# A graph layer on one core: index preparation and rows of h moved into the first pass, and nine passes of other sizes in place of seven

## The chip, the core and the metric

The kernel runs on one core of one Trainium2 chip. The metric is the device time of one execution in microseconds. PE is the matrix engine, DVE the vector engine, ACT the scalar engine, POOL the GpSimd engine; SP only issues DMAs here. PE, DVE, ACT and SP each run a list in the order in which it was written; a DMA that an engine issues stands in that list too.

## What is computed

```python
def _L0_gnn_ref(x, f_ij, rcut_ij, idx_i, idx_j, W_in2f, W_f1, b_f1, W_f2, b_f2, W_o1, b_o1, W_o2, b_o2):
    def smu(x, alpha=0.01, mu=2.5):
        return ((1 + alpha) * x + (1 - alpha) * x * erf(mu * (1 - alpha) * x)) / 2
    h = x @ W_in2f.T
    Wij = smu(f_ij @ W_f1.T + b_f1) @ W_f2.T + b_f2
    Wij = Wij * rcut_ij[:, None]
    x_ij = h[idx_j] * Wij
    agg = jax.ops.segment_sum(x_ij, idx_i, num_segments=h.shape[0])
    out = smu(agg @ W_o1.T + b_o1) @ W_o2.T + b_o2
    return out
h = jnp.maximum(_layernorm(x, axis=-1), 0.0)
x = x + _L0_gnn_ref(h, edge_attr_20, edge_weight, src, dst, ...)
```

There are 12,500 nodes with 128 features, 400,000 edges with 20 features each, and everything is float32. dst (idx_j, the node whose row of h is read) comes sorted; src (idx_i, the node that the message is added to) is random.

## The kernel before

The nodes lie in 98 bins of 128 (NB). The edges lie in 3125 tiles of 128 (NT), four of which are a group (GRP, 782 groups), eight a supertile (SUP, 391 of them). The supertiles are divided into passes by PARTS (line 32), six of 59 and one of 37; the code calls a pass an epoch. Every pass has a buffer of its own in DRAM with CAP slots for each bin: the mean number of edges that fall into a bin plus 5.8 standard deviations, rounded up to 128. Q is CAP / 128: 6 for a pass of 59, 4 for one of 37. Slots from ZMIN on may stay unused, and are filled with zeros beforehand (clear, line 152).

For a group of four tiles the loop does this. load (line 367) fetches for each supertile the edge features, the row of relative dst indices (rel_dram, which the kernel wrote itself) and 128 rows of h from h_dram. h is kept as three bfloat16 parts. bins, count, read and number find for each edge the slot in the bin of its src. hide, bend, smooth and weigh are the filter network. pick, gather and take read the rows of h through a one-hot matrix, mix multiplies the two, turn transposes, and send scales by the edge weight and scatters the messages: one indirect DMA on POOL for each tile (line 562), 3125 in all, each of 128 rows of 129 floats.

While pass k scatters, pass k-1 is summed. begin and fetch (lines 624 and 576) read the buffer back in chunks of up to 12 times 128 slots on SP's queue, choose (line 587) makes a one-hot matrix for a chunk on DVE, and add (line 598) does one 128 x 128 x 128 matrix product for each bin and each of its Q parts and adds four bins at once into agg. Here such a product is called a sum; it stands as two matrix instructions in the profile. begin comes with the second group of a pass, the first choose with its third, the first sums with its fifth (WAIT, line 634), and the sums of a pass are spread evenly over its other groups. DVE, PE and ACT wait in order, so what stands behind a choose waits with it. Meanwhile the buffer of the next pass is cleared from SP's queue, in about 50 DMAs.

After the last group the last pass has nothing to run beside: its 98 bins are summed, and for each unit of four bins the output network runs (half and rest, lines 318 to 341), with x read again and the result written from ACT's queue. rest of a unit comes in the middle of the next four bins, half at their end.

Ahead of the loop stands the preparation (lines 216 to 313): all of dst, src and the weights come in whole, on ACT's queue; the rest of x comes on POOL's. rel is made for all tiles, transposed on PE and written to rel_dram; hi_b and lo_b (bin and place in the bin of each src) are made for all edges; and the first eight bins (HEAD, line 168) get layer norm, ReLU and the product with W_in, so that their rows of h stand in h_dram. The dst of the first pass lie in these bins. The rows of the other 90 bins are made inside the first pass: others (line 661) yields steps, and step takes one at three places of every group (two statistics and two empty steps in turn, then the deviations, then six steps for every four bins).

A message tile ms has six buffers, so ACT and DVE may run up to six groups ahead of POOL.

Of the kernel before, what the change touches and what calls it, by code (L numbers as in the profile page):

```python
# [11 lines left out]
I32 = mybir.dt.int32  # L12
# [19 lines left out]
PARTS = (59, 59, 59, 59, 59, 59, 37)  # L32
# [7 lines left out]
def gnn_kernel(  # L40
# [85 lines left out]
    nc.vector.memset(onesb, 1.0)  # L126
    bad = const.tile([P, 4 + 2 * EPOCHS], F32, name="bad")
    nc.vector.memset(bad, 0.0)
# [39 lines left out]
    HEAD = 8  # L168
# [47 lines left out]
    with tc.tile_pool(name="prep", bufs=1) as prep, \  # L216
            tc.tile_pool(name="node", bufs=3) as node, \
            tc.tile_pool(name="nps", bufs=2, space=PSUM) as nps:
        dst_i = prep.tile([P, NT], I32, name="dst_i")
        src_i = prep.tile([P, NT], I32, name="src_i")  # L220
        nc.scalar.dma_start(dst_i, dst_col)
        nc.vector.memset(x_sb[:, NB - 1, :], 0.0)
        nc.sync.dma_start(x_sb[:, 0:HEAD, :], bin_rows(x, 0, HEAD))
        nc.sync.dma_start(w_in, w_in_t)
        for a, n in chunks(NB - 1 - HEAD, 30):
            nc.gpsimd.dma_start(x_sb[:, HEAD + a:HEAD + a + n, :], bin_rows(x, HEAD + a, n))
        nc.gpsimd.dma_start(x_sb[:LASTB, NB - 1, :], x[(NB - 1) * P:N, :])
        nc.scalar.dma_start(src_i, src_col)
        nc.scalar.dma_start(w_sb, w_col)
        nc.vector.memset(w_f1, 0.0)  # L230
        nc.scalar.dma_start(w_f1[0:R, :], w_f1_t)
        nc.scalar.dma_start(w_f1[R:R + 1, :], b_f1)
        nc.scalar.dma_start(w_f2, w_f2_t)
        nc.scalar.dma_start(w_o1, w_o1_t)
        nc.scalar.dma_start(w_o2, w_o2_t)
        nc.scalar.dma_start(b1, b_o1.rearrange("o p -> p o"))
        nc.scalar.dma_start(b2row, b_f2)
        nc.scalar.dma_start(b2, b_f2.rearrange("o p -> p o"))
        nc.scalar.dma_start(bo2, b_o2.to_broadcast([P, P]))

        nc.vector.memset(zero, 0.0)
        clear(0, len(cleans) - 1, nc.sync)
        zero_b = prep.tile([P, 3 * D], BF, name="zero_b")
        nc.vector.memset(zero_b, 0.0)
        nc.scalar.dma_start(h_dram[NB * P:N + WIN, :], zero_b[:N + WIN - NB * P, :])


        nc.vector.tensor_copy(base_i[:, :], dst_i[0:1, 0:NT:SUP])
        base_f = prep.tile([1, NS], F32, name="base_f")
        nc.vector.tensor_copy(base_f, base_i)  # L250
        rel = prep.tile([P, NT], F32, name="rel")
        nc.vector.tensor_copy(rel, dst_i)
        S = GRP * P // SUP
        for a, n in chunks(NS, S):
            pb = nps.tile([P, S, SUP], F32, name="pb")
            nc.tensor.matmul(pb[:, :n], ones1, base_f[:, a:a + n].unsqueeze(2).to_broadcast([1, n, SUP]),
                             start=True, stop=True)
            w = min(NT - a * SUP, n * SUP)
            nc.vector.tensor_sub(rel[:, a * SUP:a * SUP + w], rel[:, a * SUP:a * SUP + w],
                                 pb.rearrange("p s t -> p (s t)")[:, :w])  # L260
        for a, m in chunks(NT // P, GRP) + [(NT // P, 0)]:
            pd = nps.tile([P, GRP, P], F32, name="pd")
            rb = node.tile([P, GRP, P], BF, name="rb")
            if m:
                for j in range(m):
                    nc.tensor.transpose(pd[:, j, :], rel[:, (a + j) * P:(a + j + 1) * P], ident)
                nc.scalar.activation(rb[:, :m], pd[:, :m], AF.Copy)
                nc.sync.dma_start(rel_dram[0, a * P * P:(a + m) * P * P].rearrange("(c t e) -> t c e", t=P, e=P),
                                  rb[:, :m])
            elif NT % P:  # L270
                m = NT % P
                nc.tensor.transpose(pd[:m, 0, :], rel[:, a * P:NT], ident)
                nc.scalar.activation(rb[:m, 0], pd[:m, 0], AF.Copy)
                nc.sync.dma_start(rel_dram[0, a * P * P:].rearrange("(t e) -> t e", e=P), rb[:m, 0])
        lh = prep.tile([P, 2], F32, name="lh")
        nc.vector.tensor_reduce(lh[:, 0:1], rel, op=ALU.min, axis=AX.X)
        nc.vector.tensor_reduce(lh[:, 1:2], rel, op=ALU.max, axis=AX.X)
        nc.vector.tensor_scalar(bad[:, 0:1], lh[:, 0:1], 0.0, None, op0=ALU.is_lt)
        nc.vector.tensor_scalar(bad[:, 1:2], lh[:, 1:2], float(WIN - 1), None, op0=ALU.is_gt)
        most = prep.tile([1, 1], F32, name="most")  # L280
        early = eps_of[0][1] + 3
        nc.vector.tensor_reduce(most, base_f[:, :early], op=ALU.max, axis=AX.X)
# [13 lines left out]
        for b in range(HEAD):  # L296
            stats(node, b)
# [45 lines left out]
    with tc.tile_pool(name="ld", bufs=4) as ld, \  # L343
# [291 lines left out]
        for s in range(3):  # L635
            load(s)
        for s in range(2):
            pick(s)
# [266 lines left out]
```

## Time and profile before

| | us |
|---|---|
| three runs: median (lowest, highest) | 4286.98 (4285.12, 4287.03) |
| the profiled execution, its own time | 4295.33 |
| its span, first to last instruction | 4293.6 |
| first scatter starts | 93.53 |
| last scatter starts | 4094.83 |

| engine | busy us | share of the span |
|---|---|---|
| PE | 3745.7 | 87% |
| DVE | 3177.7 | 74% |
| POOL | 3029.8 | 71% |
| ACT | 2825.2 | 66% |

A row of groups reads: line, engine, operation, what is written from what, times how often, then busy time, mean duration in ns, and the idle time before it with its main cause. A row in order of time reads: start, duration, engine, line, operation, and in brackets how long the engine had been idle and what ended that. A row of stretches reads: from:to, length, then busy time and number of instructions for PE, PE's weight loads, DVE, ACT and POOL, the clock granted to PE, the busy share of the DMA engines and GB/s. POOL's time does not count what lies between two of its DMA instructions. DMA issues are printed with a q behind the engine's name.

### The profile page before, as it was taken

The page shows a single profiled execution, that of the slowest core. Times are in us where ns is not written, and L with a number is a line of the kernel's source. Part 1 is how long each engine was busy: PE and PEld are TensorE (multiplying, and loading weights), DVE is VectorE, ACT ScalarE, POOL GpSimd, SP SyncE. Part 2 cuts the span into 40 slices and gives each one's busy share as a digit, 9 for nine tenths or more (in the row PEclk, how much of TensorE's full clock was granted, in tenths as well). Part 3 has the DMA queues.
Part 4 walks back from the last instruction along what each step waited for, and adds up shares of the span by engine and source line. Part 5 has one row for each costly group of instructions (what it writes and reads, how often), then busy time and mean ns, then how long its engine had stood idle before and what let it go on. Part 6 is the DMA issues. An engine that isn't in the chain of part 4 may idle for free.

```text
span 4293.6 us, 74022 instructions
## 1 busy us (share of the span) xinstructions
PE 3745.7 (87%) x18332; PEld 2305.2 (54%) x18596; DVE 3177.7 (74%) x8458; ACT 2825.2 (66%) x11054; POOL 3029.8 (71%) x3137
## 2 busy tenths in 40 slices
PE   4877786999997999979999979999889999799977
PEld 2334443655554655545655546555556555466666
DVE  5876675877776877768877768777678777688856
ACT  2777786776766777657766667767667767566610
POOL 1777677777777777777777777777777777777710
PEclk9999998999999999989999999999999999899989
DMA  6955565766665766647666657666576666466666
GB/s 186 218 144 165 162 185 150 204 208 197 196 180 182 211 207 195 202 148 209 208 201 196 197 164 213 195 198 202 146 205 197 188 183 187 145 204 197 192 192 179
DMA packets 457334, 808.89 MB, mean 188 GB/s; under 512 B 82228, under 2 KB 258630, under 8 KB 456512
## 3 DMA queue, kind: packets, MB, share of 16 engines
q1 hardware_dynamic: 328136, 573.65, 47.4%
q0 software_dynamic: 101504, 212.48, 15.5%
q10 hardware_dynamic: 27256, 17.94, 1.4%
q8 instruction: 150, 2.46, 0.3%
q14 instruction: 288, 2.36, 0.2%
HBM read 449.68 MB, written 354.07 MB: 187 GB/s over the span
## 4 chain that ended last, share of the span: by engine, by line
PE 33%; DMA 15%; DVE 13%; ACT 5%; issue 3%; POOL 1%; ACTq 0%; DVEq 0%; POOLq 0%; SPq 0%
DMA buf<-ms,ix 13%; PE pw L529 8%; PE pg L607 8%; PE pu L479 6%; PE ph L510 5%; PE pt L549 4%; DVE se L594 4%; DVE mt L539 2%; DMA hg<-in_x 2%; ACT ms L559 2%; DVE sm L495 1%; ACT ge L487 1%; ACT jk L457 1%; DVE co L414 1%; DVE agg L620 1%
## 5 line engine op out<-in xcount | busy, mean ns | idle before, releaser
L562 POOL DMA_INDIRECT buf<-ms,ix x3125 | 3023.1, 967 | 1065.4 <-issue 278.4
L559 ACT ACTIVATE ms<-pt,w_sb 128x128 f32<-128x128 f32 x3125 | 905.0, 390 | 501.9 <-DMA buf<-ms,ix 287.0
L607 PEld LDWEIGHTS pg<-se,rw 128*128 128x128 f32 x7840 | 1075.3, 193 | 168.2 <-issue 23.4
L607 PE MATMUL pg<-se,rw 128*128 128x128 f32 x7840 | 1098.7, 276 | 19.7 <-DVE se L594 19.7
L457 ACT ACTIVATE jk<-pc,nbig 128x98 f32<-128x98 f32 x3125 | 1029.3, 354 | 12.9 <-PE pc L428 12.5
L529 PE MATMUL pw<-sm,w_f 128*128 128x512 f32 x1564 | 897.5, 656 | 27.1 <-DVE sm L495 19.6
L539 DVE SCALAR_TENSOR_TENSOR mt<-pw,b,hg 128x512 f32<-128x512 f32 x782 | 583.8, 747 | 416.7 <-ACT hg L518 414.2
L479 PE MATMUL pu<-f,w_f 128*128 128x512 f32 x1564 | 808.1, 599 | 2.6 <-DVE sm L495 2.5
L549 PE MATMUL pt<-ident,mt 128*128 128x128 f32 x3125 | 497.6, 282 | 347.3 <-DVE mt L539 343.8
L487 ACT ACTIVATE ge<-pu 128x512 f32<-128x512 f32 x782 | 469.4, 600 | 471.9 <-PE pu L479 459.9
L594 DVE TENSOR_TENSOR se<-irow_ps,rw 128x1536 f32<-128x1536 f32 x327 | 571.8, 1749 | 162.0 <-DMA rw<-buf 135.8
L457 ACT ACTIVATION_READ_ACCUMULATOR jk<-pc,nbig 128x1 f32 x3125 | 682.9, 219 | 0.0
L495 DVE SCALAR_TENSOR_TENSOR sm<-pu,ge 128x512 f32<-128x512 f32 x782 | 536.1, 686 | 186.0 <-ACT ge L487 175.2
L510 PE MATMUL ph<-oh,hw 128*128 128x512 bf16 (+1 forms) x2082 | 635.2, 387 | 15.5 <-issue 2.0
L518 ACT ACTIVATE hg<-ph 128x512 f32<-128x512 f32 x782 | 469.4, 600 | 228.8 <-PE ph L510 226.8
L549 PEld LDWEIGHTS pt<-ident,mt 128*128 128x128 f32 x3125 | 352.5, 142 | 439.3 <-DVE mt L539 434.5
L414 DVE TENSOR_TENSOR co<-co,po 128x98 f16<-128x98 f16 x2351 | 502.3, 214 | 81.2
L510 PEld LDWEIGHTS <-hw 128*128 128x128 bf16 x2346 | 234.2, 100 | 560.6 <-issue 460.0
L400 DVE TENSOR_TENSOR po<-irow_ps,hi_b 128x392 f16<-128x392 f32 x782 | 433.9, 555 | 0.0
L529 PEld LDWEIGHTS pw<-sm,w_f 128*128 128x128 f32 x1564 | 237.7, 191 | 170.7 <-DVE sm L495 167.1
L427 PE MATMUL pc<-co,ones_h 128*128 128x392 f16 x782 | 257.7, 330 | 14.0 <-DVE co L414 14.0
L479 PEld LDWEIGHTS pu<-f,w_f 128*128 128x128 f32 x1564 | 250.4, 194 | 23.6 <-DVE sm L495 4.1
(114 smaller groups left out, 1675.2 us busy)
## 6 DMA issues: line engine op xcount, KB each, us to landing
rw<-buf SPq DMA_DIRECT2D x326, 774.0 KB
buf<-zero SPq DMA_DIRECT2D x294, 387.0 KB
rbc<-rel_dram SPq DMA_DIRECT2D x390, 256.0 KB
buf<-ms,ix POOLq DMA_INDIRECT x3125
hw<-h_dram SPq DMA_DIRECT2D x391, 96.0 KB
f<-in_f_t SPq DMA_DIRECT2D x390, 80.0 KB
buf<-zero SPq DMA_DIRECT2D x49, 258.0 KB
h_dram<-hs SPq DMA_DIRECT2D x24, 384.0 KB
```

The costliest lines, as they stand in the source:

```text
L414: nc.vector.tensor_add(co[:, j], co[:, j - 1], po[:, j - 1])
L457: nc.scalar.activation(jk, pc[:, j], AF.Relu, bias=nbig, accum_out=sl[:, j:j + 1])
L479: nc.tensor.matmul(pu[:, :n], w_f1, loaded[g // PER][0][:, o:o + n], start=True, stop=True)
L495: nc.vector.scalar_tensor_tensor(sm[:, :n], units_of.pop(g)[:, :n], LIN, hidden[g][:, :n], op0=ALU.mult, op1=ALU.add)
L510: nc.tensor.matmul(ph[:, :n], hw[:, q * D:(q + 1) * D], oh[:, o:o + n], start=(q == 0), stop=(q == 2))
L529: nc.tensor.matmul(pw[:, :n], w_f2, hidden.pop(g)[:, :n], start=True, stop=True)
L539: nc.vector.scalar_tensor_tensor(mt[:, :n], pws.pop(g)[:, :n], b2, rows_of.pop(g)[:, :n], op0=ALU.add, op1=ALU.mult)
L549: nc.tensor.transpose(pt[:, j, :], mt[:, j * P:(j + 1) * P], ident)
L559: nc.scalar.activation(ms[:, j, 0:P], pt[:, j], AF.Copy, scale=w_sb[:, t + j:t + j + 1])
L562: i = nc.gpsimd.indirect_dma_start(out=bufs[k][:, :], out_offset=bass.IndirectOffsetOnAxis(ap=ix[:, j:j + 1], axis=0), in_=ms[:, j, :], in ...
L594: nc.vector.tensor_tensor(se[:, :m], irow_ps.unsqueeze(1).to_broadcast([P, m, P]), rows_in[c][:, :m, P:P + 1].to_broadcast([P, m, P]), op= ...
L607: nc.tensor.matmul(pgs[0][:, g, :], rows_in[c][:, o, 0:P], sel[c][:, o, :], start=(q == 0), stop=(q == Q[k] - 1))
```

## The change

PARTS becomes nine passes of 59, 59, 59, 59, 48, 37, 27, 27 and 16 supertiles. HEAD becomes 4. The separate preparation goes. Its work on indices is cut into seven chunks of 512 tiles (head_of): the first chunk and the four head bins are done ahead of the loop, now inside the hand-written order; the other six chunks are steps of others, each followed by the statistics of a bin, and all the steps of others are spread evenly over all but the last twelve groups of the first pass. The order ahead of the loop is changed so that one group's slots, not two groups', are found before the first weigh. The rest of x and of the weights come on ACT's queue, before ACT's first activation. The zero rows behind h_dram and the output bias become steps too, and the two range checks on rel are gathered from the chunks at the end.

With the same rule for CAP, Q becomes 6, 6, 6, 6, 5, 4, 3, 3, 2, and the cleared slots of a bin 384 in the first five passes and 256 in the last four.

```diff
@@ -29,7 +29,7 @@
 SUP = 8
 GRP = 4
 WIN = 128
-PARTS = (59, 59, 59, 59, 59, 59, 37)
+PARTS = (59, 59, 59, 59, 48, 37, 27, 27, 16)
 SIGMA = 5.8
 ROW = P + 1
 BIG = 32768.0
@@ -124,7 +124,11 @@
     nc.vector.memset(nbig, -BIG)
     onesb = const.tile([P, P], F32, name="onesb")
     nc.vector.memset(onesb, 1.0)
+    CH = 4 * P
+    NC = (NT + CH - 1) // CH
     bad = const.tile([P, 4 + 2 * EPOCHS], F32, name="bad")
+    lh = const.tile([P, 2, NC], F32, name="lh")
+    b1w = const.tile([P, P], F32, name="b1w")
     nc.vector.memset(bad, 0.0)
@@ -165,7 +169,7 @@
-    HEAD = 8
+    HEAD = 4
     BY = 44
     x_sb = agg.rearrange("p (b d) -> p b d", d=D)
     mv = const.tile([P, NB, 2], F32, name="mv")
@@ -212,105 +216,6 @@
         kept = [None]
         return [normed, turned, cut, product, first_part, other_parts]
-    with tc.tile_pool(name="prep", bufs=1) as prep, \
-            tc.tile_pool(name="node", bufs=3) as node, \
...
-        nc.scalar.dma_start(dst_i, dst_col)
-            nc.gpsimd.dma_start(x_sb[:, HEAD + a:HEAD + a + n, :], bin_rows(x, HEAD + a, n))
-        nc.vector.tensor_copy(rel, dst_i)
-        for a, m in chunks(NT // P, GRP) + [(NT // P, 0)]:
...
@@ -351,12 +256,116 @@
         irow_ps = ps1.tile([P, GRP * P], F32, name="irow_ps")[:, 0:P]
         nc.vector.tensor_copy(irow_ps, irow)
         NF = 4
-        fbufs = []
+        fbufs = [ld.tile([P, SUP * P], F32, name=f"f{i}", bufs=1) for i in range(NF)]
+        def fill(i):
+            nc.vector.memset(fbufs[i], 1.0)
+        hs = edge.tile([P, GRP, 3, D], BF, name="hs", bufs=1)
+        early = eps_of[0][1] + 3
+        def bank(name):
+            return ps2.tile([P, GRP, P], F32, name="pg")
+        def head_of(c):
+            a, n = c * CH, min(CH, NT - c * CH)
+            s0, m = a // SUP, (n + SUP - 1) // SUP
+            rw = rowp.tile([P, ROWS, ROW], F32, name="rw").rearrange("p q r -> p (q r)")
+            di, si, rel = rw[:, 0:n].bitcast(I32), rw[:, CH:CH + n].bitcast(I32), rw[:, 2 * CH:2 * CH + n]
+            if c:
+                rb = hs[:, :, 0, :]
+            else:
+                rb = edge.tile([P, SUP * P], BF, name="oh", bufs=3)[:, :CH].rearrange("p (j e) -> p j e", e=P)
+            base_f = edge.tile([1, CH // SUP], F32, name="base_f")
+            cells = [(j * P, min(P, n - j * P)) for j in range((n + P - 1) // P)]
+            kept = [None]
+            def fetched():
+                nc.sync.dma_start(di, dst_col[:, a:a + n])
+                nc.sync.dma_start(si, src_col[:, a:a + n])
+            def based():
+                nc.vector.tensor_copy(base_i[:, s0:s0 + m], di[0:1, 0:n:SUP])
+                nc.vector.tensor_copy(base_f[:, :m], base_i[:, s0:s0 + m])
+                nc.vector.tensor_copy(rel, di)
+            def spread():
+                pb = kept[0] = bank("pb")
+                flat = pb.rearrange("p j e -> p (j e)")[:, :m * SUP].rearrange("p (s t) -> p s t", t=SUP)
+                nc.tensor.matmul(flat, ones1, base_f[:, :m].unsqueeze(2).to_broadcast([1, m, SUP]),
+                                 start=True, stop=True)
+            def lowered():
+                nc.vector.tensor_sub(rel, rel, kept[0].rearrange("p j e -> p (j e)")[:, :n])
+            def turned():
+                pd = kept[0] = bank("pd")
+                for j, (o, w) in enumerate(cells):
+                    nc.tensor.transpose(pd[:w, j, :], rel[:, o:o + w], ident)
+            def written():
+                w = cells[-1][1]
+                whole = len(cells) - (w < P)
+                if whole:
+                    nc.scalar.activation(rb[:, :whole], kept[0][:, :whole], AF.Copy)
+                    nc.sync.dma_start(rel_dram[0, a * P:(a + whole * P) * P].rearrange("(c t e) -> t c e", t=P, e=P),
+                                      rb[:, :whole])
+                if w < P:
+                    nc.scalar.activation(rb[:w, whole], kept[0][:w, whole], AF.Copy)
+                    nc.sync.dma_start(rel_dram[0, (a + whole * P) * P:(a + n) * P].rearrange("(t e) -> t e", e=P),
+                                      rb[:w, whole])
+            def limits():
+                nc.vector.tensor_reduce(lh[:, 0, c:c + 1], rel, op=ALU.min, axis=AX.X)
+                nc.vector.tensor_reduce(lh[:, 1, c:c + 1], rel, op=ALU.max, axis=AX.X)
+            def bounded():
+                most = edge.tile([1, 1], F32, name="most")
+                nc.vector.tensor_reduce(most, base_f[:, :early], op=ALU.max, axis=AX.X)
+                nc.vector.tensor_scalar(bad[0:1, 2:3], most, float(HEAD * P - WIN), None, op0=ALU.is_gt)
+                nc.vector.tensor_scalar(base_i[:, :early], base_f[:, :early], float(HEAD * P - WIN), None, op0=ALU.min)
+            def binned():
+                nc.vector.tensor_scalar(di, si, 7, None, op0=ALU.arith_shift_right)
+                nc.vector.tensor_copy(hi_b[:, a:a + n], di)
+            def placed():
+                nc.vector.tensor_scalar(di, si, P - 1, None, op0=ALU.bitwise_and)
+                nc.vector.tensor_copy(lo_b[:, a:a + n], di)
+            return dict(fetched=fetched, based=based, spread=spread, lowered=lowered, turned=turned, written=written,
+                        limits=limits, bounded=bounded, binned=binned, placed=placed)
+        one = head_of(0)
+        one["fetched"]()
+        nc.scalar.dma_start(x_sb[:, 0:HEAD, :], bin_rows(x, 0, HEAD))
+        nc.scalar.dma_start(w_in, w_in_t)
+        nc.vector.memset(w_f1, 0.0)
+        nc.scalar.dma_start(w_f1[0:R, :], w_f1_t)
+        nc.scalar.dma_start(w_f1[R:R + 1, :], b_f1)
+        nc.scalar.dma_start(w_f2, w_f2_t)
+        nc.scalar.dma_start(b2, b_f2.rearrange("o p -> p o"))
+        nc.scalar.dma_start(w_sb[:, 0:CH], w_col[:, 0:CH])
         for i in range(NF):
-            fb = ld.tile([P, SUP * P], F32, name=f"f{i}", bufs=1)
-            nc.vector.memset(fb, 1.0)
-            fbufs.append(fb)
+            fill(i)
+        nc.vector.memset(zero, 0.0)
+        clear(0, len(cleans) - 1, nc.scalar)
+        nc.vector.memset(x_sb[:, NB - 1, :], 0.0)
+        for a, n in chunks(NB - 1 - HEAD, 31):
+            nc.scalar.dma_start(x_sb[:, HEAD + a:HEAD + a + n, :], bin_rows(x, HEAD + a, n))
+        nc.scalar.dma_start(x_sb[:LASTB, NB - 1, :], x[(NB - 1) * P:N, :])
+        nc.scalar.dma_start(w_sb[:, CH:NT], w_col[:, CH:NT])
+        nc.scalar.dma_start(w_o1, w_o1_t)
+        nc.scalar.dma_start(w_o2, w_o2_t)
+        nc.scalar.dma_start(b1, b_o1.rearrange("o p -> p o"))
+        nc.scalar.dma_start(b2row, b_f2)
+        nc.scalar.dma_start(bo2, b_o2.to_broadcast([P, P]))
         groups = [(t0 + a, g) for t0, nt in sups for a, g in chunks(nt, GRP)]
         NG = len(groups)
         PER = SUP // GRP
@@ -370,7 +379,8 @@
             t0, nt = sups[s]
             e0, n = t0 * P, nt * P
             fb = fbufs[s % NF]
-            nc.sync.dma_start(fb[0:R, :n], f_t[:, e0:e0 + n])
+            if s > 2:
+                nc.sync.dma_start(fb[0:R, :n], f_t[:, e0:e0 + n])
             rb = ld.tile([P, SUP * P], BF, name="rbc")
             nc.sync.dma_start(rb[:, :n], rel_dram[:, e0:e0 + n].to_broadcast([P, n]))
             hw = ld.tile([P, 3 * D], BF, name="hw")
@@ -633,48 +643,92 @@
         WAIT = 4
         for s in range(3):
+            nc.sync.dma_start(fbufs[s][0:R, :], f_t[:, s * SUP * P:(s + 1) * SUP * P])
+        one["based"]()
+        one["spread"]()
+        one["bounded"]()
+        one["lowered"]()
+        one["turned"]()
+        one["written"]()
+        nc.vector.tensor_scalar(w_f2, w_f2, GC, None, op0=ALU.mult)
+        for b in range(HEAD):
+            stats(edge, b)
+        deviations(0, HEAD)
+        rw = rowp.tile([P, ROWS, ROW], F32, name="rw")
+        for step in rows_of_h(0, HEAD, *[rw[:, j * GRP:(j + 1) * GRP, 0:P] for j in range(3)], hs, bank):
+            step()
+        for s in range(3):
             load(s)
-        for s in range(2):
-            pick(s)
-        for g in range(3):
-            bins(g)
-        count(0)
-        read(0)
-        count(1)
-        read(1)
-        number(0)
+        one["binned"]()
+        bins(0)
         hide(0)
         bend(0)
         smooth(0)
         hide(1)
         bend(1)
         weigh(0)
+        count(0)
+        read(0)
+        one["placed"]()
+        pick(0)
         gather(0)
+        number(0)
         take(0)
         mix(0)
         smooth(1)
+        bins(1)
+        count(1)
+        read(1)
+        pick(1)
+        bins(2)
         cleared = at_first = done = 0
         work = []
-        hs = edge.tile([P, GRP, 3, D], BF, name="hs", bufs=1)
+        def zeroed():
+            zr = edge.tile([P, 3 * D], BF, name="zr", bufs=1)
+            nc.vector.memset(zr, 0.0)
+            nc.sync.dma_start(h_dram[NB * P:N + WIN, :], zr[:N + WIN - NB * P, :])
+        def output_bias():
+            nc.vector.tensor_scalar(w_o2, w_o2, GC, None, op0=ALU.mult)
+            nc.vector.tensor_scalar(bz, b1, ZS, None, op0=ALU.mult)
+            nc.vector.tensor_scalar(b1w, onesb, b1, LIN, op0=ALU.mult, op1=ALU.mult)
+            pb1 = bank("pb1")[:, 0, :]
+            nc.tensor.matmul(pb1, b1w, w_o2, start=True, stop=True)
+            nc.vector.tensor_add(bo2, bo2, pb1)
         def others():
-            for b, n in chunks(NB - HEAD, 2):
-                yield lambda b=b, n=n: [stats(edge, HEAD + b + j) for j in range(n)]
-                yield None
-                yield None
+            yield one["limits"]
+            yield zeroed
+            left = list(range(HEAD, NB))
+            for c in range(1, NC):
+                it = head_of(c)
+                for name in ("fetched", "based", "spread", "lowered", "turned", "written", "binned", "placed", "limits"):
+                    yield it[name]
+                    if left:
+                        yield lambda b=left.pop(0): stats(edge, b)
+            while left:
+                two, left = left[:2], left[2:]
+                yield lambda two=two: [stats(edge, b) for b in two]
             yield lambda: deviations(HEAD, NB)
             for b, n in chunks(NB - HEAD, GRP):
                 rw = rowp.tile([P, ROWS, ROW], F32, name="rw")
                 four = [rw[:, j * GRP:(j + 1) * GRP, 0:P] for j in range(3)]
-                yield from rows_of_h(HEAD + b, n, *four, hs, lambda name: ps2.tile([P, GRP, P], F32, name="pg"))
+                yield from rows_of_h(HEAD + b, n, *four, hs, bank)
+            yield output_bias
+        COUNT = 2 + 18 * (NC - 1) + (NB - HEAD - 9 * (NC - 1) + 1) // 2 + 1 + 6 * -(-(NB - HEAD) // GRP) + 1
         h_steps = others()
+        taken_steps = slot = 0
         def step():
-            f = next(h_steps, None)
-            if f:
-                f()
+            nonlocal taken_steps, slot
+            slot += 1
+            while taken_steps < COUNT and taken_steps * 3 * (eps_of[0][1] * PER - 12) < slot * COUNT:
+                next(h_steps)()
+                taken_steps += 1
         for g in range(NG):
             s = g // PER
@@ -727,7 +781,7 @@
             bins(g + 3)
             parts(k - 1, hi)
             step()
-            assert k == 0 or next(h_steps, None) is None
+            assert k == 0 or taken_steps == COUNT and next(h_steps, None) is None
         k = EPOCHS - 1
         begin(k)
         choose(k, 0)
@@ -765,6 +819,11 @@
         open_halves(True)
     with tc.tile_pool(name="fps", bufs=1, space=PSUM) as fps:
+        ends = const.tile([P, 2], F32, name="ends")
+        nc.vector.tensor_reduce(ends[:, 0:1], lh[:, 0], op=ALU.min, axis=AX.X)
+        nc.vector.tensor_reduce(ends[:, 1:2], lh[:, 1], op=ALU.max, axis=AX.X)
+        nc.vector.tensor_scalar(bad[:, 0:1], ends[:, 0:1], 0.0, None, op0=ALU.is_lt)
+        nc.vector.tensor_scalar(bad[:, 1:2], ends[:, 1:2], float(WIN - 1), None, op0=ALU.is_gt)
         bs = const.tile([P, 1], F32, name="bs")
         nc.vector.tensor_reduce(bs, bad, op=ALU.add, axis=AX.X)
         pn = fps.tile([P, 1], F32, name="pn")
```

More of the change, by code (lines that the diff above doesn't have):

```diff
@@ L214, in rows_of_h @@
         return [normed, turned, cut, product, first_part, other_parts]
-    with tc.tile_pool(name="prep", bufs=1) as prep, \
-            tc.tile_pool(name="node", bufs=3) as node, \
-            tc.tile_pool(name="nps", bufs=2, space=PSUM) as nps:
-        dst_i = prep.tile([P, NT], I32, name="dst_i")
-        src_i = prep.tile([P, NT], I32, name="src_i")
-        nc.scalar.dma_start(dst_i, dst_col)
[L222 to L225, printed above, removed]
-            nc.gpsimd.dma_start(x_sb[:, HEAD + a:HEAD + a + n, :], bin_rows(x, HEAD + a, n))
[L227 to L251, printed above, removed]
-        nc.vector.tensor_copy(rel, dst_i)
[L253 to L260, printed above, removed]
-        for a, m in chunks(NT // P, GRP) + [(NT // P, 0)]:
[L262 to L282, printed above, removed]
-        nc.vector.tensor_scalar(bad[0:1, 2:3], most, float(HEAD * P - WIN), None, op0=ALU.is_gt)
-        nc.vector.tensor_scalar(base_i[:, :early], base_f[:, :early], float(HEAD * P - WIN), None, op0=ALU.min)
-        for a, n in chunks(NT, 625):
-            part = node.tile([P, 625], I32, name="part")
-            nc.vector.tensor_scalar(part[:, :n], src_i[:, a:a + n], 7, None, op0=ALU.arith_shift_right)
-            nc.vector.tensor_copy(hi_b[:, a:a + n], part[:, :n])
-            part = node.tile([P, 625], I32, name="part")
-            nc.vector.tensor_scalar(part[:, :n], src_i[:, a:a + n], P - 1, None, op0=ALU.bitwise_and)
-            nc.vector.tensor_copy(lo_b[:, a:a + n], part[:, :n])
-        for b in range(HEAD):
-            stats(node, b)
-        deviations(0, HEAD)
-        for b, n in chunks(HEAD, GRP):
-            four = [node.tile([P, GRP, P], F32, name=f"four{i}") for i in range(3)]
-            for step in rows_of_h(b, n, *four, node.tile([P, GRP, 3, D], BF, name="hs"),
-                                  lambda name: nps.tile([P, GRP, P], F32, name=name)):
-                step()
-        nc.vector.tensor_scalar(w_f2, w_f2, GC, None, op0=ALU.mult)
-        nc.vector.tensor_scalar(w_o2, w_o2, GC, None, op0=ALU.mult)
-        nc.vector.tensor_scalar(bz, b1, ZS, None, op0=ALU.mult)
-        b1w = prep.tile([P, P], F32, name="b1w")
-        nc.vector.tensor_scalar(b1w, onesb, b1, LIN, op0=ALU.mult, op1=ALU.mult)
-        pb1 = nps.tile([P, GRP, P], F32, name="pd")[:, 0, :]
-        nc.tensor.matmul(pb1, b1w, w_o2, start=True, stop=True)
-        nc.vector.tensor_add(bo2, bo2, pb1)
```

## Prediction

> **What bounds the kernel now.** I read the page first (busy table, costliest groups), then the stretches by pass, then the order of time at the start, at a pass boundary and at the end.
>
> ```profile
> span 4293.6 us, 74022 instructions
> ...
> L562 POOL DMA_INDIRECT buf<-ms,ix x3125 | 3023.1, 967 | 1065.4 <-issue 278.4
> ```
>
> PE is busiest (87%), but the pace is POOL's. It issues 3125 scatters; each takes 967 ns, and 0.30 us passes before the next (the POOL rows below). 3125 x 1.27 = 3969 us is the floor of the loop; it ran from 93.53 to 4095.8, 4002 us. So the time is **front 93.5 + loop 4002 + tail 197.8**, and only 33 us of the loop is loss.
>
> ```profile
> core 0: us, PE busy (x) PEld busy (x) DVE busy (x) ACT busy (x) POOL busy (x), PEclk, DMA share, GB/s
> ...
> 425.00:572.00 147.00, 115.48 (x453) 60.46 (x460) 101.35 (x307) 104.81 (x379) 98.23 (x97) 0.93 0.54 159
> ...
> 719.00:1319.00 600.00, 540.11 (x2671) 332.73 (x2711) 452.13 (x1201) 415.83 (x1652) 456.09 (x472) 0.98 0.66 194
> ...
> 3717.00:4096.00 379.00, 357.57 (x2050) 249.72 (x2084) 304.26 (x740) 246.88 (x966) 282.61 (x294) 0.98 0.65 194
> 4096.00:4294.00 198.00, 147.94 (x1034) 131.49 (x1034) 120.34 (x137) 17.19 (x26) 0.00 (x0) 0.89 0.66 196
> ```
>
> Second row: pass 1, 472 scatters (59 supertiles, 118 groups of four) in 600 us, 5.08 us a group, without a gap; every full pass is like it. First row: inside pass 0, 97 scatters where 116 would fit: 25 us lost while rows of h are made (POOL waits for ACT at L208 there). Third row: the 37-supertile pass, 5.15 us a group, 5 us lost: PE is full there. Last row: the tail.
>
> **Front.**
>
> ```profile
> 30.36 0.49 DVE L176 BATCH_NORM_STATS2 st<-agg 128x6 f32<-128x128 f32 x2 [27.71 <-DMA agg<-in_x]
> ...
> 36.92 1.28 ACT L267 ACT_TABLE_LOAD   x1 [36.92 <-DMA w_o<-in_w_o_t]
> ...
> 68.22 1.17 SPq L210 DMA_DIRECT2D h_dram<-hs  x2
> 70.12 0.33 SPq L373 DMA_DIRECT2D f<-in_f_t  x1
> 70.50 0.50 SPq L375 DMA_DIRECT2D rbc<-rel_dram  x1
> ...
> 93.53 1.04 POOL L562 DMA_INDIRECT buf<-ms,ix  x1 [86.25 <-DVE ix L466]
> ```
>
> Inputs until 36 us, then all 25 x 128 columns of indices and eight blocks of h until 70, then 23 us to the first scatter. The change reads 512 of the 3125 index columns and four blocks of x first, and does the rest in pass 0. But all of x now goes out on ACT's queue ahead of ACT's first activation, and eight DMA semaphores are used in turn: in the changed program's list, the first write of rel_dram waits for the third big x transfer, and the first read of it for the rest of w_sb. Ahead of x lie dst, src, w_sb (256 KB each), x's head, weights, three f and one clear: 1.8 MB. Stretches of 2 us before showed 360 to 405 GB/s up to 18 us and about 290 in x's share, so 2 + 4.8 us, then 6.1 MB of x at 290 = 21, to 28 us; w_sb's 1.3 MB brings 32. ACT is free at 21 us (second x transfer landed) to 31 (its queue is full until the last issue). From there: table load 1.3, rb 0.6, table load 1.3, rstd 0.3, and the chain from four to h_dram that took 7.8 us for two sets (60.38 to 68.22), 6.5 for one: h written at 31 to 41, loads at 34 to 43. What follows is shortened too (one group's bins and count, not three and two, precede the first weigh): 17 us by my walk over the rows, 23 by the row before. First scatter at 34 + 17 = 51 up to 64; I take 53.5, nearest the early end, as the queue's landings release ACT: **-40** (-30 to -44).
>
> **Rest of pass 0.** Before, 138 row steps go in 46 groups, three a group; a set (two groups) cost 1.5 us over POOL's pace, and POOL lived 100 us on its lead before it starved at 425. After, 276 steps (index chunks and statistics first) are spread over 106 groups, 2.6 a group, the 144 row steps over the last 55. With 4.05 us for a group that has only statistics (mt at 95.10, 99.22, 103.19) and 5.83 with three row steps, a step costs 0.6 us; 2.6 give 5.6, so 55 x 0.5 = 28 minus a lead of about 12: 16 lost in place of 25, **-8** after rounding. Against it: each of six chunks adds 4 us of DVE (cast, subtract, four conversions, two reductions by the rows at 32 to 55 us, scaled to 512 of 3125 columns), and DVE waits for a chunk two slots after SP issued it, behind clears on SP's queue. At 5 us of wait each, that is 30 us against a lead of 1 us per group: from -20 to +20.
>
> **Passes of falling size.** Slots per bin (Q) become 6,6,6,6,5,4,3,3,2, 41 in place of 40; clears rise from 2560 to 2944 slots a bin. What counts is the sums per group: before 588/114 = 5.2, in the last pass 588/70 = 8.4. After: 5.2, 6.4, 7.0, 7.8, 5.9 and, in the last pass of 16 supertiles, 294/28 = 10.5. On PE a group without sums takes 3.16 us and a sum 0.222 (three sets of four or five took 0.89 to 1.11 between 4050.8 and 4058.9). So 7.8 sums: 4.90, still under 5.08, nothing lost; 10.5: 5.49, and with the 0.12 that 8.4 sums lost on top of their 5.03, 5.6. 28 x 0.52 = 15 against the 5 lost before: **+10** (0 to 25; DVE there needs 2.9 + 10.5 x 0.146 + the adds into agg = 5.0, close behind).
>
> Two more boundaries:
>
> ```profile
> 720.23 2.33 SPq L583 DMA_DIRECT2D rw<-buf  x4
> 725.60 1.76 DVE L594 TENSOR_TENSOR se<-irow_ps,rw 128x1536 f32<-128x1536 f32 x1 [20.59 <-DMA rw<-buf]
> ```
>
> DVE stood 20.6 us, yet POOL's rows go on every 1.27 us: it has two groups of the new pass in hand until 729.3, and DVE was free at 727.4. The margin is under 2 us. The Trainium skill ("TensorE: Matmul & The Clock Gate", "What's actually happening") says that an idle window of about 3.4 us halves PE's clock until it has been busy as long again; the stretch 719 to 754 shows it, granted clock 0.82. By the rule an added boundary costs up to 1.7 us of PE, and so do those of the passes with no slack; by the row none, as POOL does not starve. With fuller DMA (clears at one a group, about 235 GB/s in the first 27-pass) I put **+3** (0 to 15).
>
> **Tail.**
>
> ```profile
> 4120.76 0.46 ACTq L323 DMA_DIRECT2D hg<-in_x  x1
> ...
> 4128.80 0.69 DVE L335 TENSOR_TENSOR ms<-pw,hg 128x512 f32<-128x512 f32 x1 [4.46 <-DMA hg<-in_x]
> 4129.52 0.69 DVE L336 TENSOR_TENSOR ms<-ms,bo 128x512 f32<-128x512 f32 x1
> 4130.24 0.39 ACTq L338 DMA_DIRECT2D out<-ms  x1
> 4130.73 0.47 ACTq L323 DMA_DIRECT2D hg<-in_x  x1
> ```
>
> Each unit of four bins waits for its x, adds twice, sends out, and only then is the next x issued: landing + 1.95 us. From 4120.76 to 4271.38 there are 21 rounds, 7.17 us each. Halving the sums (Q 4 to 2) takes 8 x 0.222 = 1.8 us of PE from a unit, but x stays; on the chain it takes 5.5 to 6 us, 3.85 at least. The skill ("DMA: Bandwidth & Descriptors", "Anatomy of one DMA") would give 2.0 us + bytes/436 GB/s = 2.6 us; x would then be off the path, a round would be ge, sm, pw, two adds and two issues, 5.5 us, and 35 us be won. The row decides; with half as much fetched beside it I take 4.35: 6.3 a round, 21 x 0.87 = 18, and 5 for the first two sets of bins (16 sums in place of 32, which took 10.3): **-23** (-5 to -35).
>
> **Sum.** -40 - 8 + 10 + 3 - 23 = -58 on the span of 4293.6; its run took 4295.33, the median is 4286.98. 4287 - 58 = **4229**.
>
> **Rivals.** A, as summed: 0.58, own range 4212 to 4246. B, the tail hangs on x as before (landing 5.7, 7.65 a round; only the first 5 us are won): 4229 + 18 = 4247; for it, 14 x landings are the longest pieces of the tail's chain; against, the rounds at 4233 and 4254 with 3.85: 0.18. C, the front's work is only moved: chunks starve POOL in pass 0, +20 in place of -8, 4257; for it, the DMA share of 0.94 at 100 to 200 us: 0.12. D, slower: holes at the pass boundaries. If the first fetch of a pass takes 15 us in place of 5.4 because clears and scatters crowd the DMA engines, each of eight boundaries opens 9.6 us: 4226 + 77 = 4303; it passes the old time from holes of 7.6 us. For it, the margin of 2 us; against, a DMA share of 0.82 at 719 to 754, not 1: 0.12, of which 0.07 slower. That the front does not shorten because of the semaphores named (first scatter at 64) stays in A's range, 4240.
>
> 0.2% (9 us) is about what can be told from no change. Faster 0.88, within 0.05, slower 0.07; range 4202 (all early ends but one) to 4262 (C with some of B).
>
> **What would show it.** First scatter near 53; ACT's first table load at 21 to 31; fewer than 19 scatters missing in pass 0; 125 scatters of the last pass at 1.4 us each; no gap of POOL over 2 us at boundaries; x issues 6.3 us apart in the tail. Wrong if POOL shows gaps in every short pass, or if ACT starts after 36.

## The result

The changed kernel takes **4248.6 us** (median of four runs, 4247.0 to 4252.1) against 4286.05 for the kernel before: ratio 0.9915, 95% interval 0.9897 to 0.9932. The forecast was 4229, range 4202 to 4262. The profiled execution took 4248.45, its span is 4246.6; so this profile stands at its median, whereas the one of before stands 8 to 9 above.

The start, on the timeline of the changed kernel (start, duration, engine and line; in brackets the idle time before and who ended it):

```profile
8.00 0.83 ACTq L360 DMA_DIRECT2D agg<-in_x  x1
...
9.29 6.69 ACTq L360 DMA_DIRECT2D agg<-in_x  x1
...
10.78 1.09 PE L308 MATMUL pg<-ident,rw 128*128 128x128 f32 x4 [0.87 <-DVE w_f L653]
...
16.44 6.33 ACTq L360 DMA_DIRECT2D agg<-in_x  x1
22.86 6.89 ACTq L361 DMA_DIRECT2D agg<-in_x  x1
29.79 0.38 ACTq L362 DMA_DIRECT2D w_sb<-in_w_col  x1
...
32.32 0.33 ACTq L367 DMA_DIRECT2D bo<-in_b_o  x1
32.68 1.28 ACT L314 ACT_TABLE_LOAD   x1 [16.27 <-DMA agg<-in_x]
...
43.61 0.41 SPq L214 DMA_DIRECT2D h_dram<-hs  x1
44.11 0.45 SPq L385 DMA_DIRECT2D rbc<-rel_dram  x1
...
58.58 1.11 POOL L572 DMA_INDIRECT buf<-ms,ix  x1 [57.01 <-ACT ms L569]
```

The first scatter starts at 58.58 in place of 93.53. ACT writes no tile until its table load at 32.7, 0.03 us after the end of its last issue (32.32 + 0.33). What its first activation reads was ready long before: PE had turned the first chunk of rel (L308) by 11.9. The first of the four x issues takes 0.83 us, the other three stand in ACT's list for 6 to 7 us each. Their own size does not set that: three of the transfers have 2 MB, the last (L361) 42 KB and 6.89 us, and the 1.3 MB of w_sb behind it take 0.38. An issue waits for what is ahead of it. From the table load it is 11 us to the write of h and 15 more to the scatter.

Stretches of the same trace (length; busy time and count of PE, PEld, DVE, ACT, POOL; granted clock; DMA share; GB/s): inside pass 0, pass 1, both passes of 27 supertiles, the pass of 16, and the tail:

```profile
480.00:630.00 150.00, 118.46 (x469) 58.80 (x476) 107.86 (x330) 112.52 (x426) 107.60 (x110) 0.98 0.62 176
678.00:1277.00 599.00, 544.64 (x2672) 335.18 (x2711) 452.13 (x1201) 417.07 (x1652) 455.24 (x472) 0.98 0.66 194
3343.00:3618.00 275.00, 260.75 (x1441) 177.20 (x1468) 227.07 (x565) 185.09 (x730) 204.64 (x213) 0.98 0.92 237
3618.00:3893.00 275.00, 252.58 (x1267) 157.92 (x1288) 216.80 (x568) 191.45 (x752) 205.82 (x215) 0.99 0.77 212
3893.00:4070.00 177.00, 162.44 (x961) 115.51 (x972) 141.48 (x333) 106.22 (x412) 125.42 (x130) 0.97 0.65 190
4070.00:4247.00 177.00, 110.91 (x642) 92.32 (x642) 93.32 (x121) 17.20 (x26) 0.00 (x0) 0.83 0.51 145
```

Read the count of POOL: 110 scatters in 150 us of pass 0, where 118 fit (97 of 116 before); 472 in a full pass, as before; 213 and 215 in 275 us, where 217 fit; 130 in the 177 us of the last pass, where PE is busy for 162. In the tail PE falls to 111 of 177 us and its clock to 0.83.

At a pass boundary DVE waits for the first fetch; the two lines are of the list of waits, the kernel before first (waits in all, times, longest):

```profile
DVE se L594 <- DMA rw<-buf: 135.8, 8, 21.3
```

```profile
DVE se L604 <- DMA rw<-buf: 125.2, 10, 20.7
```

Two boundaries more, and no more waiting. POOL's largest gap after its first scatter is 2.8 us, in pass 0; in the 40 us behind each boundary none is over 1.9. Stretches of 35 us from the boundaries at 677.9 and 3342.7 on, in the columns of above:

```profile
677.00:712.00 35.00, 24.59 (x110) 14.45 (x112) 22.40 (x57) 18.07 (x72) 26.49 (x28) 0.80 0.81 250
...
3342.00:3377.00 35.00, 24.54 (x118) 15.49 (x121) 22.70 (x56) 16.06 (x62) 26.47 (x29) 0.79 0.86 249
```

PE is idle for 10 of the 35 us and its mean granted clock is 0.8, but POOL issues 28 and 29 scatters, and 35 us at 1.267 hold 27.6.

The tail, on the timeline of the changed kernel:

```profile
4109.11 0.39 ACTq L243 DMA_DIRECT2D out<-ms  x1
4109.54 0.52 ACTq L228 DMA_DIRECT2D hg<-in_x  x1
...
4115.10 0.69 DVE L240 TENSOR_TENSOR ms<-pw,hg 128x512 f32<-128x512 f32 x1 [1.86 <-DMA hg<-in_x]
4115.82 0.69 DVE L241 TENSOR_TENSOR ms<-ms,bo 128x512 f32<-128x512 f32 x1
4116.55 0.39 ACTq L243 DMA_DIRECT2D out<-ms  x1
4116.98 0.52 ACTq L228 DMA_DIRECT2D hg<-in_x  x1
```

It is the same round as before: x issue, landing (5.6 us here), two adds, out, next x issue, 7.44 us for this one. Others take 5.5, where x has landed before PE is done. Over 21 rounds the mean is 6.40, against 7.17 (second to 23rd issue of both).

**Where the time went.** The starts of the scatters that begin and end a pass divide each span. In the last three columns, which the experiments below explain, two kernels that each hold one half of the change ran on one chip. The last column is their difference, the kernel that holds the half named in brackets minus the one that does not:

| piece, us | before | after | difference | short front alone | nine passes alone | difference that each half makes there |
|---|---|---|---|---|---|---|
| to the first scatter | 93.5 | 58.6 | -35.0 | 57.0 | 91.6 | -34.6 (front) |
| pass 0 | 625.7 | 619.3 | -6.4 | 614.5 | 623.2 | -8.7 (front) |
| passes 1 to 3 | 1799.2 | 1800.0 | +0.7 | 1794.2 | 1795.8 | -1.6 (front) |
| later passes, to the last scatter | 1576.4 | 1591.1 | +14.7 | 1574.3 | 1580.0 | +5.7 (passes) |
| from the last scatter to the end | 198.8 | 177.7 | -21.1 | 192.7 | 177.3 | -15.4 (passes) |
| span | 4293.6 | 4246.6 | -47.0 | 4232.7 | 4267.9 | |

The spans differ by 47, the medians by 37.4: each column is one execution, and the profiled one of before lies 8 to 9 above its median.

On two of the four chips that the experiments ran on, every kernel, the one before included, took 5250 to 5380 us, with engines standing still for some us now and then; totals from there tell little of the change, and only pieces that recur everywhere are used from them ("a chip with halts" below).

### The profile page after: what moved, and what is told of

Its sections match the earlier page's. It is cut to its first block, busy times and chain, and to the rows that moved or that the text cites. A ratio compares the mean times of both kernels' runs of the same rounds, so it can differ in the third digit from the quotient of the medians.

```text
span 4246.6 us, 74532 instructions
## 1 busy us (share of the span) xinstructions
PE 3736.8 (88%) x18497; PEld 2320.1 (55%) x18794; DVE 3220.9 (76%) x8578; ACT 2830.2 (67%) x11057; POOL 3017.8 (71%) x3133
## 5 line engine op out<-in xcount | busy, mean ns | idle before, releaser
L617 PEld LDWEIGHTS pg<-se,rw 128*128 128x128 f32 x8036 | 1096.5, 193 | 158.6 <-issue 21.2
L617 PE MATMUL pg<-se,rw 128*128 128x128 f32 x8036 | 1118.7, 276 | 10.4 <-DVE se L604 10.4
L539 PE MATMUL pw<-sm,w_f 128*128 128x512 f32 x1564 | 883.5, 647 | 40.6 <-DVE sm L505 35.4
L604 DVE TENSOR_TENSOR se<-irow_ps,rw 128x1536 f32<-128x1536 f32 (+1 forms) x345 | 587.5, 1703 | 145.8 <-DMA rw<-buf 125.2
```

What stands on the lines that cost most here:

```text
L539: nc.tensor.matmul(pw[:, :n], w_f2, hidden.pop(g)[:, :n], start=True, stop=True)
L604: nc.vector.tensor_tensor(se[:, :m], irow_ps.unsqueeze(1).to_broadcast([P, m, P]), rows_in[c][:, :m, P:P + 1].to_broadcast([P, m, P]), op= ...
L617: nc.tensor.matmul(pgs[0][:, g, :], rows_in[c][:, o, 0:P], sel[c][:, o, :], start=(q == 0), stop=(q == Q[k] - 1))
```

## The experiments

The twelve runs below were spread over four chips, each beside the kernel before on the same chip. They are told by subject, not in order of time: the kernel with both x loads moved ran before the four single edits were run again.

**The short front alone.** The changed kernel with the old passes:

```diff
-PARTS = (59, 59, 59, 59, 48, 37, 27, 27, 16)
+PARTS = (59, 59, 59, 59, 59, 59, 37)
```

> The new front with the old seven passes. Theory (the pieces add up: front -35, rest of pass 0 -6, late passes +15, tail -21): first scatter at 58.6, pass 0 in 619, last pass of 37 in 377, tail 199; 6 us above the changed kernel, about 4255. Rival (the gain comes from the falling passes, the front only moves its work): at 4275 or above, pass 0 longer than 626.

It ran on a chip with halts: 5312 against 5318 there, ratio 0.9983 (0.9962 to 1.0005). Its first scatter was at 57.57 and its tail 195.9: the pieces that the theory names, with the total unreadable. Run again:

> The kernel before with the short front alone, its seven passes kept (again, on a chip on which the kernel before runs at its usual time). Theory (the parts add: front -35, pass 0 -6): first scatter at 57 to 59, pass 0 some 619, the rest as before, so some 4243 (4235 to 4252). Rival (the gain of the front is given back in pass 0, which now runs beside more transfers): pass 0 above 640, and the time within 15 us of before.

4238.4 against 4282.5, ratio 0.9904 (0.9887 to 0.9920): -44. First scatter at 57.0, pass 0 614.5. The front's gain is kept, and pass 0 (expected 619) gains besides; the rival falls.

**The nine passes alone.** The kernel before, with the converse edit:

> The old front with the new nine passes. Theory: first scatter at 93.5, the five late passes 15 us over the old two, tail 178 in place of 199; 6 us under the kernel before, about 4280. Rival (the tail is won and the short passes cost nothing beside the old front): 4265. Rival (holes at the boundaries of short passes): above 4290.

On the chip with halts: 5374, ratio 1.0086 (1.0053 to 1.0119); first scatter 92.67, tail 177.6. Again:

> The kernel before with the nine falling passes alone, its own front kept. Theory (late passes +15, tail -21 on the spans): first scatter at 93 to 94, pass 0 some 625, last scatter about 15 later than in before, tail about 178, so some 6 us faster than before, 4278 (4270 to 4288), hardly to be told from it. Rival (the falling sizes carry the gain of the pair): 20 us or more faster.

4271.5, ratio 0.9976 (0.9967 to 0.9986): -11. First scatter at 91.6, tail 177.3, and the later passes 5.7 longer than with the old sizes on that chip. So of the two halves the front carries most of the gain, and the passes a small part of it. Together they make -55 there.

**The kernel before as it is**, on that chip, for the pieces:

> The kernel before, unchanged, for a second profile: its profiled execution took 4295, its median run 4286. Theory: front, passes and last scatter agree within 2 us (POOL paces them), and the 9 us lie in the tail, where the x transfers vary. Rival: the 9 us lie in the front (input transfers) or in pass 0.

One run took 5310.2. First scatter 94.14, tail 196.0, as on the other chips; but pass 0 took 779 and a pass of 59 some 752 in place of 600. The loop is not at POOL's pace there, so nothing said of the passes can be tested on that chip, and where the 9 us of the first profile lie is not answered.

**x of the front from POOL.** The front's theory is that ACT comes free when its queue has room, not when data are there. The kernel before had issued these same loads from POOL.

```diff
         for a, n in chunks(NB - 1 - HEAD, 31):
-            nc.scalar.dma_start(x_sb[:, HEAD + a:HEAD + a + n, :], bin_rows(x, HEAD + a, n))
-        nc.scalar.dma_start(x_sb[:LASTB, NB - 1, :], x[(NB - 1) * P:N, :])
+            nc.gpsimd.dma_start(x_sb[:, HEAD + a:HEAD + a + n, :], bin_rows(x, HEAD + a, n))
+        nc.gpsimd.dma_start(x_sb[:LASTB, NB - 1, :], x[(NB - 1) * P:N, :])
```

> The changed kernel with the rest of x issued from POOL, as before the change, so that ACT's list holds no big transfer but the rest of w_sb ahead of its first activation. Theory (ACT's full queue set the front): ACT's first table load at 10 to 14 in place of 32.7, first scatter at 36 to 44, time 15 to 22 less than the changed kernel, about 4230. Rival (the data set it: index rows and weights share the DMA engines with 6.1 MB of x until 30): first scatter not before 52, time within 6 of the changed kernel.

On the chip with halts: 5341, ratio 1.0007 (0.9971 to 1.0043), so the total says nothing; but the first scatter came at 43.78, and ACT's table load at 17.1, later than the 10 to 14 expected. Again:

> The changed kernel with the later x transfers of the front issued by POOL in place of ACT, again. Theory (the term that the prediction mis-sized is when ACT comes free: its list is held by the x issues): ACT's first table load at 17 to 20 in place of 32.7, first scatter at 43 to 45 in place of 58.6, the rest unmoved: 4248.6 - 15 = about 4234 (4226 to 4242). Rival (an earlier first scatter meets chunks that aren't there, and pass 0 gives it back): pass 0 above 630 and the time above 4244.

4211.0, ratio 0.9838 (0.9822 to 0.9855). Its timeline at the start:

```profile
1.57 5.48 POOL L360 DMA_DIRECT2D agg<-in_x  x3
...
16.94 0.34 ACTq L367 DMA_DIRECT2D bo<-in_b_o  x1
17.31 1.28 ACT L314 ACT_TABLE_LOAD   x1 [17.31 <-DMA b2row<-in_b_f]
...
28.24 0.41 SPq L214 DMA_DIRECT2D h_dram<-hs  x1
...
43.84 1.04 POOL L572 DMA_INDIRECT buf<-ms,ix  x1 [35.42 <-ACT ms L569]
```

POOL issues three x transfers in 5.5 us; on ACT all but the first stood 6 to 7 each. ACT starts 15.4 us earlier, the scatter 14.7 earlier, and pass 0 does not give it back (616.2). The time is 23 below the 4234 expected and outside its range: the front is as expected, and the pieces put the rest into the loop (later passes 1579 against 1591; see below).

**x of the tail from POOL.** Its line in the tail's helper:

```diff
         xr, ge, sm, ys = tiles
+        queue = nc.gpsimd if queue is nc.scalar else queue
```

> The changed kernel with the x loads of the tail issued by POOL in place of ACT. Theory (a tail round is ACT's list: its work, the out issue and the x issue, which waits for room): rounds from 6.4 to about 5.1, the tail from 178 to about 147, the rest unmoved: 4248.6 - 31 = about 4218 (4210 to 4228). Rival (the gain of the tail in the combined kernel came from its last pass of 17 or from the front): rounds above 6, time above 4238.

4199.6, ratio 0.9810 (0.9793 to 0.9826). The tail took 144.8, 32.9 less than 177.7, on this timeline:

```profile
4094.03 0.75 POOL L229 DMA_DIRECT2D hg<-in_x  x1 [4.17 <-DVE ms L241]
4094.50 0.38 ACTq L244 DMA_DIRECT2D out<-ms  x1
...
4097.70 0.69 DVE L241 TENSOR_TENSOR ms<-pw,hg 128x512 f32<-128x512 f32 x1 [1.31 <-PE pw L240]
4098.43 0.69 DVE L242 TENSOR_TENSOR ms<-ms,bo 128x512 f32<-128x512 f32 x1
4098.69 0.75 POOL L229 DMA_DIRECT2D hg<-in_x  x1 [3.91 <-DVE ms L241]
```

x is asked for when the first add has freed its buffer, ahead of the out and not behind it; it has landed when PE is done 3.7 us later. The round is 5.01 us in the mean of 21, and DVE waits for PE. The lines of the list of waits in the tail show the same, the changed kernel first:

```profile
DVE ms L240 <- DMA hg<-in_x: 26.0, 11, 3.2
...
DVE ms L240 <- PE pw L239: 17.4, 13, 2.2
```

```profile
DVE ms L241 <- PE pw L240: 20.3, 16, 1.8
```

No line of waits for x is left. The total went 18 below the 4218 expected and outside its range; again most of that is in the loop, since the tail won 33 where 31 was expected.

**The last passes a little evener**, 26 and 17 in place of 27 and 16:

```diff
-PARTS = (59, 59, 59, 59, 48, 37, 27, 27, 16)
+PARTS = (59, 59, 59, 59, 48, 37, 27, 26, 17)
```

> The changed kernel with the last three passes of 27, 26 and 17 supertiles in place of 27, 27 and 16 (the same 391 supertiles in all). Theory (a pass of 16 pays its sums at the finer grain with less pass behind it, 5.47 us a supertile against 5.14 in the pass before): the last pass goes from 169.6 to about 181, the one before from 277 to about 265, and with a tail of one size the time is within 5 us of the changed kernel. Rival (the last pass's size sets the tail's start): over 8 us to either side.

It ran on the second chip with halts: 5288, ratio 1.0006 (0.9976 to 1.0037), with 221.1 us in its last pass against 210.4. No verdict from this. But the next kernel holds the same edit on a chip without them.

**Both x loads from POOL, and 26 and 17.**

> Three edits on the changed kernel: the rest of x issued from POOL at the start, x of the tail issued from POOL (which is idle there) in place of ACT's queue behind the result of the unit before, and the last two passes 26 and 17 supertiles in place of 27 and 16. Theory (ACT's queue set the front, the x transfer the rounds of the tail, sums per group the last pass): first scatter near 44, rounds of the tail 5.4 to 5.8 in place of 6.4, last pass 3 to 5 us less over POOL's pace; 30 us under the changed kernel, about 4218. Rival (pass 0 has no lead to spare, so a shorter front is lost in it, and the rounds of the tail are PE's and DVE's chain): within 8 us of the changed kernel, about 4245.

4179.4, ratio 0.9756 (0.9740 to 0.9772). First scatter 43.86, pass 0 613.5, tail 144.7. About 4218 was expected; it came 39 lower, as the rounds of the tail fell to 5.0 where 5.4 to 5.8 was expected and the loop ran quicker too. Its last two passes took 264.2 and 181.1, as forecast for them (265 and 181), but its last four (37, 27, 26, 17) took 1094.0, those of the kernel with the tail's x alone 1096.9 and those of the kernel with the front's x alone 1092.3: so the sizes 26 and 17 bring nothing that shows, where 3 to 5 us was expected. This is the fastest of the kernels, 69 us below the changed one by the medians of different chips. The two moves of x account for 14.7 + 33.0 on the pieces; of the remaining 21 us, the later passes hold 10.4 and pass 0 and passes 1 to 3 hold 10.4.

**The changed kernel and the kernel before, again.** The two halves together had given -55 where the change itself gave -37, so both were to be measured on one chip:

> The changed kernel unaltered, on a chip and in a call of its own with the kernel before, as the two parts run alone gave -44 and -11 us there, together -55, where the changed kernel had given -37 in its own comparison. Theory (the parts add, and the missing 18 us were the spread of the loop between chips and executions, some 0.2 us in each of the 59-supertile passes and more in the last ones): here some 4230 (4222 to 4240), 45 to 60 below before. Rival (the two parts get in each other's way): 30 to 42 below before, as in the first comparison.

> The kernel before unaltered, for a second profile of it beside the changed kernel's, on the same chip. Both theories: first scatter 93 to 94, tail 196 to 199, about 4283. If its passes of 59 supertiles take as long here as the changed kernel's (within 1 us each), then the loop's own spread, and not the change, was in the difference between the two first profiles.

Both went to the second chip with halts: 5306.9, ratio 1.0037 (1.0011 to 1.0062), and 5278.4, ratio 0.9998 (0.9964 to 1.0033). Front and tail are as on every chip (57.4 and 94.0; 179 and 196), but the later passes took 2031 and 1942, one execution each: nine passes cost far more there than the 6 to 15 us of the other chips, and the change as a whole loses. The first chip with halts shows the same: 2056 and 2080 with nine passes, 1983 and 1997 with seven. The question which these two were to settle, what the unaltered change takes beside its halves on one chip, stays open.

## Why the prediction was right

The total lies in the range, but not where the forecast had it. 4248.6 is 2.6 above the 4212 to 4246 of the case A that was summed, and nearest to the 4247 of rival B. That nearness is luck: B has the whole miss in the tail, and there it is not. Each of the four pieces came a little short of its forecast, and a fifth term, the spread between executions, was not in the sum.

**Front: the mechanism was right and one term mis-sized.** The step bounded ACT's start from both sides, "ACT is free at 21 us (second x transfer landed) to 31 (its queue is full until the last issue)", and took the early end, "as the queue's landings release ACT". The trace shows 32.7, a little beyond the late end: each x issue behind the first took 6.3 to 6.9 us, about as long as 2 MB ahead of it take at the 290 GB/s of the forecast (7 us; the trace has 289 from 16 to 23), and the six issues behind them 3 us more. The rest of the walk was forecast longer than it was: 10.9 to the write of h (10 forecast), but 15.0 from there to the scatter (20 forecast, the loads included). So 53.5 became 58.6 and -40 became -35; the two errors partly cancel. The run with x on POOL shows the term: ACT begins 0.03 us after its last issue there too, at 17.3, and the scatter is at 43.8, ahead of the 51 to 64 of the forecast. The rival, that the data set the scatter at 52 or later, falls. What in ACT's queue runs full, bytes, packets or a count of transfers, no run tells.

**Pass 0.** Forecast -8 (16 lost in place of 25), measured -6.4 and, between the halves on one chip, -8.7. Against 472 scatters at 1.267 us, 598 us, the pass lost 28 before and 21 after. Rival C, chunks that starve POOL, did not come.

**Passes of falling size, and boundaries.** Forecast +10 for the last pass and +3 for the rest; measured +14.7 with +0.7 in passes 1 to 3, or +5.7 on one chip. The two sums agree better than their terms. The pass of 16 has its 124 intervals in 169.6 us, 1.37 each, where 1.4 was forecast from PE's count of sums (10.5 a group): 12.5 lost against POOL's 1.267, where 15 was forecast. But the last pass of before, 292 intervals in 377.4 us, lost 7.4 and not 5, so this term is +5 and not +10 (+6 on the one chip). PE is busy for 162 of the 177 us, which fits the reason given; that PE sets this pass no run tests. Boundaries cost nothing that shows, on POOL or in DVE's waits: the largest gap of POOL behind one is 1.9 us, and none over 2 was forecast. The granted clock is 0.8 at both boundaries shown, which fits the rule of the skill that the forecast named, but POOL's lead covered it, as the row had said. Rival D falls. The other 9 of the +14.7 were not forecast: they lie in the passes of 37, 27 and 27, with 377.8, 279.3 and 277.3 us, where the three kernels of the experiments with these sizes, on a chip without halts, took 374 to 375, some 275 and 273 to 275. In the first pass of 27 the DMA share is 0.92 against 0.85 there.

**Tail.** Forecast -23 (18 from rounds of 6.3, 5 from the first bins); measured 21 x (7.17 - 6.40) = 16 and 5, -21.1; between the halves on one chip -15.4. Rival B, x as late as before, is half true: 11 of the waits are still for x. The 5.5 us a round that the forecast worked out for x off the path still had both issues in it: with that of x off ACT's list the round is 5.0. The section of the skill that the forecast set against the row gives its 2.0 us + bytes/436 GB/s for DMAs issued from GpSimd, and these x loads came from ACT; the forecast was right to let the row decide. With x from POOL, where the figure belongs, x landed within the 3.7 us in which PE got done; how long before, no run tells.

**The sum.** -58 was forecast on the spans; -47 was measured: 5 of the difference are the front, 2 pass 0, 2 the passes, 2 the tail. The other 8 to 9 us between the forecast and the measured median are the 8.4 by which the profile of before lay above its median, while that of the changed kernel lies at its own: a spread between executions, which the range held and no step of the sum named.

**What stays open.** On the chip of the two halves, three estimates say what the change would have taken: 4282.5 - 44 - 11 = 4227 from the halves, 4211.0 + 14.7 = 4226 from x on POOL, 4199.6 + 32.9 = 4232 from the tail's x. The change itself took 4248.6 on its own. Its loop was the slower: the later passes 1591.1, where the four other kernels with nine passes on chips without halts took 1579 to 1584. Three of these four hold both halves, so the halves do not get in each other's way in the later passes. In the table of DMA queues (packets, MB, share of 16 engines' span), the changed kernel and then the one with the tail's x alone:

```profile
q1 hardware_dynamic: 380986, 601.70, 51.8%
```

```profile
q1 hardware_dynamic: 380986, 601.70, 49.5%
```

The same packets took 0.518 x 4246.6 = 2200 us of the engines there and 0.495 x 4199.6 = 2079 here, 6% less. Slower transfers in that execution fit the late first pass of 27, where the share was 0.92 against 0.85 in the other kernel's same stretch; that they are the cause, and that the chip and not the edit makes them, no run shows.

## What to carry to other kernels

A DMA's issue is an instruction in some engine's list. Before moving large loads to an engine that has first work to do, ask what its list holds until the queue has room; an engine that idles at that time is the place for them. In a loop of load, add and store, take the next load's issue off the list that carries the store. And a sum whose terms come to tens of us must say how far two executions of one kernel lie apart, since that is added to every difference.

## What was not expected of the hardware

Loads of x are cut up in different ways. Of the table of DMA queues, in the window 4110 to 4180 of each tail (packets, MB, share), x and out from ACT in the changed kernel, then the x loads alone from POOL:

```profile
q10 hardware_dynamic: 10944, 5.44, 26.4%
```

```profile
q0 software_dynamic: 1120, 3.67, 19.8%
```

From ACT a packet has 0.5 KB, from POOL 3.3 KB. It is not the issuing engine alone that sets this: in the front the same engine's x loads have packets of 2 KB (q10, 16 to 23 us: 1003 packets, 2.02 MB). So small packets of 0.5 KB are not what holds ACT's list there.

On the two chips with halts the kernel before ran 23 and 24% longer (5283 and 5318 against 4286). Of the timeline of the kernel before on one of them:

```profile
2398.35 0.96 POOL L562 DMA_INDIRECT buf<-ms,ix  x1 [0.30 <-issue]
...
2400.31 0.60 ACT L518 ACTIVATE hg<-ph 128x512 f32<-128x512 f32 x1 [5.25 <-remote]
2400.94 0.75 DVE L539 SCALAR_TENSOR_TENSOR mt<-pw,b,hg 128x512 f32<-128x512 f32 x1 [7.38 <-issue]
2401.74 1.11 PE L549 MATMUL pt<-ident,mt 128*128 128x128 f32 x4 [8.29 <-DVE mt L539]
```

ACT stood 5.25 us with no cause in the program, DVE and PE behind it. Such halts recur through the loop. The table of queues lists 150 and 288 packets of instruction loads over its 5263 us, and exactly as many in the usual 4294 us of the same kernel, so more loads are not the reason. The Trainium skill ("Runtime: NRT & Kernel Launch", "Instruction fetch mechanics") describes engines that stream their code in blocks, mostly hidden behind the work; whether the halts are such loads, each taking longer there, no run tells.
